# A hybrid of scan, attention and experts: the side products of the last attention loop are issued from two halves of one PSUM bank, in single bursts and at another pace

## The chip, the cores and the metric

The kernel runs on one core of a Trainium2 chip. The metric is the device time of one execution in microseconds (us). The engines are PE (TensorE: matrix products into PSUM), ACT (ScalarE), DVE (VectorE), POOL (GpSimd) and SP (SyncE, which issues most DMAs). PSUM has eight banks of 512 float32 columns in each of 128 partitions.

## The reference

Four images of 64 x 64 pixels and 128 channels pass through a state-space layer (three scans), then as 4096 tokens each through attention with a feed-forward part, then through experts that each pick tokens. What matters here comes after the scan:

```python
t = t + _L1_attn_ref(_ln_t(t), ...)        # (4, 4096, 128)
t = t + _L1_ffn_ref(_ln_t(t), ...)

# _L1_attn_ref: 16 heads of 8
scores = jnp.einsum('bhsd,bhtd->bhst', q, q) / np.sqrt(D)
attn = jax.nn.softmax(scores, axis=-1)
ctx = jnp.einsum('bhst,bhtd->bhsd', attn, q)
attn_out = ctx @ w_comb.T + b_comb
x1 = _ln(x + attn_out, g1, beta1)
zf = jnp.cos(x1[..., :8]) * jnp.cos(ry_theta)
h = jax.nn.relu(zf @ w1.T + b1)            # w1 (512, 8)
ffn_out = h @ w2.T + b2                    # w2 (128, 512)
return _ln(x1 + ffn_out, g2, beta2)

# _L1_ffn_ref: 64 experts, each picks K = 8 tokens of an image
logits = jnp.einsum('bsd,ed->bse', x, gate_w) + gate_b
probs = jax.nn.softmax(logits, axis=1)     # over the tokens
vals, idx = jax.lax.top_k(probs.transpose(0, 2, 1), K)
pooled = jnp.einsum('bked,bke->bed', gathered, topv)
# two layers per expert, weighted by topv, added to the picked tokens
```

## The kernel before

**Stages.** The scan of image 0 and the inputs of all images come first (the fill). Then attention runs image by image in four loops. Loops 0, 1 and 2 carry beside them the scan of the next image, its opening, and the closing (`after`) of the image before. The last loop has no scan left to carry. Behind it stand the closing of image 3's last block, the experts' choice for it, their answers and the scatter: the tail.

**A loop** has 1024 rounds: 32 turns (4 groups of heads by 8 blocks of 512 queries) of 32 rounds, one for each 128 keys. A round issues, in this order:
- `scores(i + 1)` (L1013): four float32r products on row tiles of 32 into two of the three two-bank tiles `s`, and two ACT exponentials of 128 x 1024 (L1018);
- `beside(i)`: side work;
- `values(i)` (L1027): four fp32 products on column tiles of 32 into the one bank `acc`.

Behind a turn's last round DVE copies `acc` to `av` (L1036), and three rounds later POOL issues the stores of the context and the sums. PSUM is full with that: six banks of scores, one `acc`, one `bank` for all side work.

**The order is written out by hand.** Each engine runs its own instructions in the order in which the program issues them, under `manual_schedule`. So a side product in PE's line whose input is late holds the values and scores behind it. Side work is a chain of generators. Each `yield PE` says that the next step is a product; `WAIT` says that a step can do nothing yet. `Pace.turn(share, free)` adds credit in each round and runs steps for it, at most one PE step a round, and none where `free` is false. The last loop's call is

```python
block.loop(nb - 1, lambda i: last.turn(1.5, i % 3 > 0 or i > 830), True)
```

`flow` keeps two pieces of work interleaved. A piece asks for PSUM with `Bank.take`, which yields `PE` once and then as long as the bank is taken; `leave` gives it back when the copy out has been issued. `pause` yields `PE` between two parts of a product, so that they stand in different rounds: a part is called a burst here, and one of two matmuls a double.

**Side work of the last loop**, in order: the closing of image 2, the choice of experts' tokens for images 0 and 1 and then 2, and the closing of image 3's first seven blocks as they become ready. A closing of a 512-token block has these products: `co` (combination of heads, L1130, 2 x 2 matmuls of 128 columns), `zt` (transpose of the cosines, L1153), `h` (first feed-forward product, L1171, 4 x 2 of 256 columns), `fo` (second, L1184, 4 x 4 of 128 columns, accumulating), `xT` (transpose, L1208) and `lg` (gate, L1222). In front of `co` stand the shares (`shares`: the sums of the exponentials are loaded, inverted, stored and loaded again) and behind `fo` two normalizations in a row (`norm`, L886 to L901). A `norm` is statistics on DVE, a power on POOL and four applications on DVE (L899); the second writes the tokens that `xT` transposes. DVE moves every product out of PSUM: h at L1174, fo at L1188. Between `co` and `zt` the cosines of all blocks of a group are formed: DVE folds the angles (`turned`), ACT takes the sine (L1241), for which it loads another function table and then the exponential's again. The choice (`choice`, L1315 to L1345) takes eight values of each row out of 4096, on DVE, in steps of some 4.4 us; the gathering (`pool`) then has for each block four `wt` matmuls (transposes weighted by the share, L1357) and four accumulating `pool` matmuls (L1368).

Of the kernel before, what the change touches and what calls it, by code (L numbers as in the profile page):

```python
# [11 lines left out]
F32 = mybir.dt.float32  # L12
# [114 lines left out]

class Bank:


# [14 lines left out]
    def leave(self):  # L145
        self.free += 1
# [582 lines left out]
class Attention:  # L729
# [3 lines left out]
    def __init__(self, tc, ctx, w, gate, cols, ident, bank, dram, t1, w_out, scans, sz, x):  # L733
# [16 lines left out]
        self.cos_ry = const.tile([D, 3], F32, name="cos_ry")  # L750
        nc.scalar.dma_start(out=self.cos_ry[:, 0:1], in_=w["ry_theta"].unsqueeze(1))
        cosine(nc, self.cos_ry[:, 2:3], self.cos_ry[:, 0:1], self.cos_ry[:, 1:2], self.half_pi)
        self.w_comb = const.tile([P, C], F32, name="w_comb")
        self.w1 = const.tile([D, FFN], F32, name="w1")
# [6 lines left out]
        with tc.tile_pool(name="a_load", bufs=1) as load, tc.tile_pool(  # L761
            name="a_load_ps", bufs=2, space=PSUM
        ) as load_ps:
            raw = load.tile([P, C], F32, name="raw_comb")
            nc.sync.dma_start(out=raw, in_=w["w_comb"])
            ps = load_ps.tile([P, 512], F32, tag="ps", name="ps_comb")
            nc.tensor.transpose(ps[:, :C], raw, ident)
            nc.vector.tensor_copy(self.w_comb, ps[:, :C])
            raw = load.tile([P, 4, D], F32, name="raw_w1")
            nc.sync.dma_start(out=raw, in_=w["w1"].rearrange("(f p) d -> p f d", p=P))  # L770
            ps = load_ps.tile([P, 512], F32, tag="ps", name="ps_w1")
            for f in range(4):
                nc.tensor.transpose(ps[:D, f * P : (f + 1) * P], raw[:, f, :], ident)
            nc.vector.tensor_copy(self.w1, ps[:D])
            raw = load.tile([P, FFN], F32, name="raw_w2")
            nc.sync.dma_start(out=raw, in_=w["w2"])
            ps = load_ps.tile([P, 512], F32, tag="ps", name="ps_w2")
            for f in range(4):
                nc.tensor.transpose(ps[:, f * P : (f + 1) * P], raw[:, f * P : (f + 1) * P], ident)
            nc.vector.tensor_copy(self.w2.rearrange("p f c -> p (f c)"), ps)  # L780
            raw = load.tile([E, C], F32, name="raw_gate")
            nc.scalar.dma_start(out=raw, in_=gate_w)
            ps = load_ps.tile([P, 512], F32, tag="ps", name="ps_gate")
            nc.tensor.transpose(ps[:, :E], raw, ident[:E, :E])
            nc.vector.tensor_copy(self.gate, ps[:, :E])
# [90 lines left out]
    def pause(self):  # L876

        if self.cut:
            yield PE

# [193 lines left out]
    def after(self, b, gs=range(L // QB), to=None):  # L1074
# [13 lines left out]
        z = self.small.tile([P, NT, D], F32, tag="z", bufs=1, name=f"z_{b}_{gs[0]}")  # L1088

# [20 lines left out]
        def first(g):  # L1110
# [15 lines left out]
            for half in range(2):  # L1126
                ps = yield from self.bank.take(f"co_{b}_{g}_{half}")
                for k in range(2):
                    at = slice((2 * half + k) * P, (2 * half + k + 1) * P)
                    nc.tensor.matmul(ps[:, k * C : (k + 1) * C], cT[:, at], self.w_comb, start=True, stop=True)  # L1130
                yield
                u_h = flat(u[:, 2 * half : 2 * half + 2, :])
                nc.vector.tensor_add(u_h, u_h, ps[:, : 2 * C])
                self.bank.leave()
# [8 lines left out]
        def second(g):  # L1143
# [5 lines left out]
            ps = yield from self.bank.take(f"zt_{b}_{g}")  # L1149
            for k in range(4):  # L1150
                if k == 2:
                    yield from self.pause()
                nc.tensor.transpose(ps[:D, k * P : (k + 1) * P], z[:, g * 4 + k, :], self.ident)  # L1153
            yield
            zT = self.piece([D, 512], "p0", name=f"zT_{b}_{g}")
            nc.vector.tensor_scalar_mul(zT, ps[:D], self.cos_ry[:, 2:3])
            self.bank.leave()
# [7 lines left out]
            for f in range(4):  # L1165
                ps = yield from self.bank.take(f"h_{b}_{g}_{f}")
                for part in range(2):
                    cols = slice(part * QB // 2, (part + 1) * QB // 2)
                    if part:
                        yield from self.pause()  # L1170
                    nc.tensor.matmul(ps[:, cols], self.w1[:, f * P : (f + 1) * P], zT[:, cols], start=True, stop=True)  # L1171
                yield
                if self.n == 2:
                    nc.vector.tensor_scalar(h[:, f, :], ps, self.b1[:, f : f + 1], 0.0, ALU.add, ALU.max)  # L1174
                else:
                    nc.scalar.activation(h[:, f, :], ps, AF.Relu, bias=self.b1[:, f : f + 1])
                self.bank.leave()
            yield from self.settle()
            for k in range(4):
                ps = yield from self.bank.take(f"fo_{b}_{g}_{k}")  # L1180
                for f in range(4):
                    if f == 2:
                        yield from self.pause()
                    nc.tensor.matmul(  # L1184
                        ps[:, :C], h[:, f, k * P : (k + 1) * P], self.w2[:, f, :], start=(f == 0), stop=(f == 3)
                    )
                yield
                nc.vector.tensor_add(u[:, k, :], u[:, k, :], ps[:, :C])  # L1188
                self.bank.leave()
# [14 lines left out]
            ps = yield from self.bank.take(f"xT_{b}_{g}")  # L1204
            for k in range(4):
                if k == 2:
                    yield from self.pause()
                nc.tensor.transpose(ps[:, k * P : (k + 1) * P], u[:, k, :], self.ident)  # L1208
            yield
            xT = self.piece([P, 512], "p0", name=f"xT_{b}_{g}")  # L1210
            nc.vector.tensor_copy(xT, ps)  # L1211
            self.bank.leave()
# [3 lines left out]
            ps = yield from self.bank.take(f"lg_{b}_{g}")  # L1216
            rows = slice(E, 2 * E) if to else slice(0, E)
            for part in range(2):
                cols = slice(part * QB // 2, (part + 1) * QB // 2)
                if part:  # L1220
                    yield from self.pause()
                nc.tensor.matmul(ps[rows, cols], self.gate, xT[:, cols], start=True, stop=True)  # L1222
            yield
            if to:
                for t in to:
                    nc.vector.tensor_scalar_add(t, ps[rows], self.gate_b[rows])
            else:
                lg = self.piece([E, 512], "p1", name=f"lgs_{b}_{g}")
                nc.vector.tensor_scalar_add(lg, ps[rows], self.gate_b[rows])
                nc.gpsimd.dma_start(out=self.logits[b][:, g * 512 : (g + 1) * 512], in_=lg)  # L1230
            self.bank.leave()
# [3 lines left out]
        def cosines():  # L1235
            turns = self.small.tile([P, NT, D], F32, tag="zturns", bufs=1, name=f"zturn_{b}_{gs[0]}")
            zs, turns = (t[:, 4 * gs[0] : 4 * blocks.stop, :] for t in (z, turns))
# [4 lines left out]
            yield  # L1242
            yield
# [10 lines left out]
class Experts:  # L1254
# [4 lines left out]
    def __init__(self, tc, ctx, ident, weight1, weight2, block, nb):  # L1259
# [14 lines left out]
        self.diagonal = const.tile([P, nb // 2, E], F32, name="diagonal")  # L1274
        self.found, self.ahead, self.rooms = {}, [], 0

    def biases(self):
# [13 lines left out]
        bank.leave()  # L1291
# [23 lines left out]
    def choice(self, images, blocks):  # L1315
# [24 lines left out]
        for b in images:  # L1340
            own = slice(b % 2 * E, b % 2 * E + E)
            nc.vector.tensor_scalar_mul(
                self.diagonal[own, b // 2, :], self.ident[own, own], self.share[own, b // 2 : b // 2 + 1]
# [4 lines left out]
    def pool(self, b, g):  # L1348

        nc, bank, rows = self.nc, self.block.bank, slice(b % 2 * E, b % 2 * E + E)  # L1350
        x = self.some.tile([P, 4, C], F32, tag="x", bufs=4, name=f"x_{b}_{g}")
        nc.sync.dma_start(out=x, in_=self.block.xn[b][:, g * 4 : g * 4 + 4, :])
        yield
        ps = yield from bank.take(f"wt_{b}_{g}")
        for i in range(4):
            at = (g * 4 + i) * P
            nc.tensor.matmul(  # L1357
                ps[:, i * E : (i + 1) * E], self.chosen[b // 2][rows, at : at + P], self.diagonal[rows, b // 2, :],
                start=True, stop=True,
            )  # L1360
        yield
        wT = self.some.tile([P, 4, E], F32, tag="wT", name=f"wT_{b}_{g}")
        nc.vector.tensor_copy(wT.rearrange("p i e -> p (i e)"), ps[:, : 4 * E])
        bank.leave()
        yield
        ps = yield from bank.take(f"pool_{b}_{g}")
        for i in range(4):
            nc.tensor.matmul(ps[:, :E], x[:, i, :], wT[:, i, :], start=(i == 0), stop=(i == 3))  # L1368
        yield
        into = self.pooled[:, :, b]  # L1370
        if g == 0:
            nc.vector.tensor_copy(into, ps[:, :E])
        else:
            nc.vector.tensor_add(into, into, ps[:, :E])
        bank.leave()
        yield

    def gather(self, images):
        yield from flow((self.pool(b, g) for b in images for g in range(NT // 4)), 2, 3)
# [157 lines left out]
def tile_kernel(tc, ctx, x, in_proj_w, dirs, out_proj_w, attn, gate, weight1, weight2, out):  # L1537
# [86 lines left out]
    with tc.manual_schedule():  # L1624
# [9 lines left out]
        block.loop(nb - 1, lambda i: last.turn(1.5, i % 3 > 0 or i > 830), True)  # L1634
# [52 lines left out]
```

## Time and profile before

| | us |
|---|---|
| median of three runs | 11369.05 |
| lowest, highest | 11349.99, 11371.47 |
| the profiled execution: time | 11359.39 |
| its span (first to last instruction) | 11357.7 |
| loop 0, from its first exponential to its last | 1997 to 4375 |
| loop 1 | 4379 to 6740 |
| loop 2 | 6747 to 9070 |
| last loop | 9073 to 11108 |
| tail | 11108 to 11358 |

The mean granted clock of PE is 0.943 of full speed. A row of the profile's groups reads: line of the kernel, engine, operation, result and operands, their shapes, count, then busy time in all, mean nanoseconds of one, and the idle time of the engine ahead of it with what ended most of it. A row of the timeline reads: start and length in us, engine, line, operation, and in brackets how long the engine had been idle and what released it. The ends of matmuls are modelled, so neighbouring rows on PE overlap a little. An fp32 matmul is recorded twice, because it is done in two passes; a float32r matmul or a transpose is recorded once.

### The profile page before, as it was taken

The page shows a single profiled execution, that of the slowest core. Times are in us where ns is not written, and L with a number is a line of the kernel's source. Part 1 is how long each engine was busy: PE and PEld are TensorE (multiplying, and loading weights), DVE is VectorE, ACT ScalarE, POOL GpSimd, SP SyncE. Part 2 cuts the span into 40 slices and gives each one's busy share as a digit, 9 for nine tenths or more (in the row PEclk, how much of TensorE's full clock was granted, in tenths as well). Part 3 has the DMA queues.
Part 4 walks back from the last instruction along what each step waited for, and adds up shares of the span by engine and source line. Part 5 has one row for each costly group of instructions (what it writes and reads, how often), then busy time and mean ns, then how long its engine had stood idle before and what let it go on. Part 6 is the DMA issues. An engine that isn't in the chain of part 4 may idle for free.

```text
span 11357.7 us, 182956 instructions
## 1 busy us (share of the span) xinstructions
PE 9864.2 (87%) x68358; PEld 3270.5 (29%) x68358; DVE 8267.2 (73%) x8405; ACT 9991.9 (88%) x10828; POOL 3757.7 (33%) x3891
## 2 busy tenths in 40 slices
PE   6697782888999889999998898999998999999995
PEld 2233331222222222222222222222222223333323
DVE  7999987888888987999998979988999221111212
ACT  4576672999999999999999999999999999989992
POOL 5887773323323223334233124243331110000000
PEclk8898895999999999999999999999999999999997
DMA  7888887556566665665656655656555332222225
GB/s 200 235 253 228 231 239 206 147 144 156 140 155 164 178 171 140 158 164 136 156 140 172 185 158 153 156 140 153 148 146 156 119 99 71 76 71 83 76 64 187
DMA packets 900978, 1747.50 MB, mean 154 GB/s; under 512 B 203150, under 2 KB 443846, under 8 KB 899830
## 3 DMA queue, kind: packets, MB, share of 16 engines
q1 hardware_dynamic: 764414, 1468.11, 48.4%
q0 software_dynamic: 93856, 156.41, 4.8%
q10 hardware_dynamic: 41816, 111.28, 3.4%
q8 instruction: 537, 8.80, 0.3%
q14 instruction: 355, 2.91, 0.1%
HBM read 1379.76 MB, written 355.47 MB: 153 GB/s over the span
## 4 chain that ended last, share of the span: by engine, by line
PE 37%; ACT 25%; issue 14%; DVE 12%; DMA 10%; POOL 1%; SPq 1%; ACTq 0%; DVEq 0%; POOLq 0%
PE acc L1027 21%; ACT e L1018 20%; PE s L1013 10%; DVE h L576 5%; DMA delta<-d_delta 4%; DMA du<-d_du 2%; PE cv L415 2%; DVE dB L566 1%; ACT dA L557 1%; ACT delta L557 1%; PE y L614 1%; PE fo L1184 1%; PE h L1171 1%; PE xd L431 1%; DMA B<-d_bc 0%
## 5 line engine op out<-in xcount | busy, mean ns | idle before, releaser
L1018 ACT ACTIVATE e<-s 128x1024 f32<-128x1024 f32 x8192 | 7777.9, 1105 | 233.1 <-PE s L1013 221.3
L1027 PE MATMUL acc<-e,val 128*32 128x512 f32 x32768 | 5255.2, 616 | 106.7 <-ACT av L1036 94.0
L1013 PE MATMUL s<-qm,key 32*128 32x512 f32 x16384 | 2648.4, 500 | 588.5 <-ACT e L1018 558.4
L1013 PEld LDWEIGHTS s<-qm,key 32*128 32x128 f32 x16384 | 1013.8, 184 | 4448.8 <-issue 2490.0
L578 POOL COPY ends<-h 128x1 f32<-128x1 f32 x1152 | 1292.6, 1123 | 2332.1 <-DVE h L576 2318.1
L566 DVE TENSOR_TENSOR dB<-du,B 128x1024 f32<-128x1024 f32 x960 | 1216.0, 1267 | 450.8 <-PE y L614 224.7
L1027 PEld LDWEIGHTS acc<-e,val 128*32 128x32 f32 x32768 | 972.6, 109 | 1608.4 <-issue 787.9
L576 DVE TENSOR_TENSOR_SCAN h<-dA,ends,dB 128x1024 f32<-128x1024 f32 x576 | 1350.4, 2344 | 110.9 <-ACT dA L557 70.7
L557 ACT ACTIVATE dA<-delta,A 128x1024 f32<-128x1024 f32 x768 | 935.6, 1218 | 421.4 <-DMA delta<-d_delta 373.7
L576 DVE TENSOR_TENSOR_SCAN h<-delta,ends,du 128x1024 f32<-128x1024 f32 x432 | 1012.3, 2343 | 127.4 <-ACT delta L557 64.8
L583 POOL TENSOR_TENSOR hC<-h,C 128x1024 f32<-128x1024 f32 x384 | 1001.1, 2608 | 160.2 <-PE y L614 85.1
L557 ACT ACTIVATE delta<-delta,A 128x1024 f32<-128x1024 f32 x768 | 937.4, 1221 | 21.6 <-DMA d_du<-u 7.1
L587 DVE TENSOR_TENSOR du<-h,C 128x1024 f32<-128x1024 f32 x576 | 701.1, 1217 | 0.1
L587 DVE TENSOR_TENSOR dB<-h,C 128x1024 f32<-128x1024 f32 x576 | 701.0, 1217 | 0.0
L566 DVE TENSOR_TENSOR du<-du,B 128x1024 f32<-128x1024 f32 x576 | 690.6, 1199 | 6.0 <-DMA B<-d_bc 5.9
L1042 POOL DMA_DIRECT2D d_ctx<-av x512 | 260.2, 518 | 1020.8 <-DVE av L1036 647.0
L415 PE MATMUL cv<-xn,conv 128*128 128x512 f32 x1024 | 472.6, 615 | 41.8 <-DVE xn L346 31.7
L608 POOL DMA_DIRECT2D d_du<-x_delta x272 | 157.2, 578 | 1012.9 <-DVE x_delta L607 951.8
L576 DVE TENSOR_TENSOR_SCAN h<-dA,dB 128x1024 f32<-128x1024 f32 x192 | 438.7, 2285 | 40.7 <-ACT dA L557 30.4
L614 PE MATMUL y<-dB,sel 128*32 128x256 f32 x4608 | 378.5, 401 | 9.5 <-DVE xT L1211 5.1
L576 DVE TENSOR_TENSOR_SCAN h<-delta,du 128x1024 f32<-128x1024 f32 x144 | 328.8, 2283 | 67.4 <-issue 34.5
L614 PE MATMUL y<-hC,sel 128*32 128x256 f32 x3072 | 239.8, 443 | 147.9 <-DVE o L630 144.6
(246 smaller groups left out, 7198.1 us busy)
## 6 DMA issues: line engine op xcount, KB each, us to landing
delta<-d_delta SPq DMA_DIRECT2D x768, 512.0 KB
du<-d_du SPq DMA_DIRECT2D x632, 512.0 KB
key<-d_q SPq DMA_DIRECT2D x352, 256.0 KB
du<-d_du ACTq DMA_DIRECT2D x136, 512.0 KB
B<-d_bc SPq DMA_DIRECT2D x96, 512.0 KB
C<-d_bc SPq DMA_DIRECT2D x96, 512.0 KB
us<-d_u SPq DMA_DIRECT2D x384, 128.0 KB
y<-d_y SPq DMA_DIRECT2D x192, 256.0 KB
```

Source lines behind the costliest of these rows:

```text
L415: nc.tensor.matmul(banks[2 * m + g], w["conv"][:, k, m * P : (m + 1) * P], reads(k, g), start=(k == 0), stop=(k == 3))
L557: nc.scalar.activation(tiles["delta", s], t, AF.Exp, scale=A)
L566: nc.vector.tensor_mul(tiles["du", s], du, spread[order, c, "B", j % 2])
L576: nc.vector.tensor_tensor_scan(h, dA, dB, first, ALU.mult, ALU.add)
L578: nc.gpsimd.tensor_copy(ends[order, c][:, at : at + 1], h[:, T - 1 :])
L583: nc.gpsimd.tensor_mul(tiles["du", s], h, spread[order, c, "C", j % 2])
L587: nc.vector.tensor_mul(dB, h, spread[order, c, "C", j % 2])
L614: nc.tensor.matmul(y[32 * g : 32 * g + 32, : T // 4], self.sel[:, j // 2, :], hC[:, 256 * g : 256 * g + 256], start=(j == 0), stop=(j == 3),)
L1013: nc.tensor.matmul(s_ps[:, k, :], keys[f"{i // 4}"][rows, cut].bitcast(F32R), queries[j, qb][rows, :].bitcast(F32R), start=True, stop=True,)
L1018: nc.scalar.activation(e, s_ps, AF.Exp, scale=1.0 / math.sqrt(D))
L1027: nc.tensor.matmul(accs[j, qb][32 * k : 32 * k + 32, :], v[:, k * VW : k * VW + 32], es[i][k // 2][:, k % 2, :], start=(kc == 0), stop=(kc ...
L1042: nc.gpsimd.dma_start(out=self.context[b][h * D : h * D + D, cut], in_=av[32 * k : 32 * k + D, :])
```

## The change

- In the last loop the side work gets `Halves` for its bank: one PSUM tile of 512 columns, handed out as two halves of 256. `take` yields `WAIT` (no longer `PE`) while no half is free, and while an accumulation is open (`summing`). `WAIT` doesn't use the PE step of a round.
- Bursts are single matmuls: `fo` pauses after each of its four matmuls, `co` and `wt` too. `pool` pauses once, after two.
- `h` becomes a float32r product with 32 rows: both factors are split into a high and a low part by a mask on the bits, and the four products of the parts are summed by one matmul of 32 rows. The weights are split at the start. The cosines are split behind ACT's sine in `cosines`, with cos(ry_theta) multiplied in there rather than at the copy of `zt`: four more DVE operations and one more `yield`. `zt` transposes 32 columns for each token tile. With a bank of 512 columns (loops 1 and 2, and the tail) one such matmul makes all of a 512-token block's `h` for 128 rows; with halves, two of 256.
- The two images of a pair are gathered together: `wt` is one matmul of 128 rows and 128 columns against a block-diagonal matrix (for a single image 64 by 64), and `pool` follows for each image.
- The pace of the last loop is 2.0 credits a round, with a PE step allowed in three rounds of four (all after 830).

The diff, cut:

```diff
 class Bank:
+    width, summing = 512, False
...
-    def leave(self):
+    def leave(self, ps=None):
+        self.free += 1
+
+class Halves(Bank):
+    width = 256
+
+    def __init__(self, whole):
+        self.parts, self.free = [whole[:, :256], whole[:, 256:]], 2
+
+    def take(self, name):
+        while True:
+            while not self.free or self.summing:
+                yield WAIT
+            yield PE
+            if self.free and not self.summing:
+                return self.grab(name)
+
+    def grab(self, name):
+        self.free -= 1
+        return self.parts.pop(0)
+
+    def leave(self, ps=None):
+        self.parts.append(ps)
         self.free += 1
...
-    def pause(self):
+    def pause(self, fresh=False):
         if self.cut:
             yield PE
+            while fresh and self.bank.summing:
+                yield WAIT
+                yield PE
...
                 for k in range(2):
+                    if k:
+                        yield from self.pause(True)
                     at = slice((2 * half + k) * P, (2 * half + k + 1) * P)
                     nc.tensor.matmul(ps[:, k * C : (k + 1) * C], cT[:, at], self.w_comb, start=True, stop=True)
...
             for f in range(4):
-                ps = yield from self.bank.take(f"h_{b}_{g}_{f}")
-                for part in range(2):
-                    cols = slice(part * QB // 2, (part + 1) * QB // 2)
-                    if part:
-                        yield from self.pause()
-                    nc.tensor.matmul(ps[:, cols], self.w1[:, f * P : (f + 1) * P], zT[:, cols], start=True, stop=True)
-                yield
-                if self.n == 2:
-                    nc.vector.tensor_scalar(h[:, f, :], ps, self.b1[:, f : f + 1], 0.0, ALU.add, ALU.max)
...
+                for col in parts_of:
+                    ps = yield from self.bank.take(f"h_{b}_{g}_{f}_{col.start}")
+                    nc.tensor.matmul(
+                        ps[:, :width], self.w1[:, f * P : (f + 1) * P].bitcast(F32R), zT[:, col].bitcast(F32R),
+                        start=True, stop=True,
+                    )
+                    yield
+                    if self.n == 2:
+                        nc.vector.tensor_scalar(h[:, f, col], ps[:, :width], self.b1[:, f : f + 1], 0.0, ALU.add, ALU.max)
...
                 for f in range(4):
-                    if f == 2:
+                    if f:
                         yield from self.pause()
+                    self.bank.summing = f < 3
...
         def cosines():
...
             nc.scalar.activation(zs, zs, AF.Sin, bias=self.half_pi, scale=-1.0)
             yield
+            yield
+            n = zs.shape[1]
+            four = parts[:, 4 * gs[0] : 4 * blocks.stop, :, :]
+            nc.vector.tensor_mul(zs, zs, self.cos_ry[:, 2, :].unsqueeze(1).to_broadcast([P, n, D]))
+            split(nc, (four[:, :, 0, :], four[:, :, 1, :]), zs)
+            nc.vector.tensor_copy(four[:, :, 2:, :], four[:, :, :2, :])
             yield
...
-    def pool(self, b, g):
+    def pool(self, images, g):
...
+        own = min(4, bank.width // n)
+        for first in range(0, 4, own):
+            ps = yield from bank.take(f"wt_{images[0]}_{g}_{first}")
+            for i in range(own):
+                at = (g * 4 + first + i) * P
+                if i:
+                    yield from pause(True)
+                nc.tensor.matmul(
+                    ps[:, i * n : (i + 1) * n], self.chosen[j][rows, at : at + P], self.diagonal[rows, j, rows],
+                    start=True, stop=True,
+                )
...
+            for i in range(4):
+                if i == 2:
+                    yield from pause()
+                bank.summing = i < 3
+                nc.tensor.matmul(ps[:, :E], x[:, i, :], wT[:, i, k * E : (k + 1) * E], start=(i == 0), stop=(i == 3))
...
-        block.loop(nb - 1, lambda i: last.turn(1.5, i % 3 > 0 or i > 830), True)
+        block.bank = Halves(bank.pool.tile([P, 512], F32, tag="bank", name="halves"))
+        block.loop(nb - 1, lambda i: last.turn(2.0, i % 4 > 0 or i > 830), True)
```

`zt`, `xT` and `lg` are cut the same way: by halves of 256 columns, each with its own `take`, copy and `leave`.

## The prediction

> **What bounds the kernel now.** First the page, for what bounds the loops:
>
> ```profile
> PE 9864.2 (87%) x68358; PEld 3270.5 (29%) x68358; DVE 8267.2 (73%) x8405; ACT 9991.9 (88%) x10828; POOL 3757.7 (33%) x3891
> ...
> L1018 ACT ACTIVATE e<-s 128x1024 f32<-128x1024 f32 x8192 | 7777.9, 1105 | 233.1 <-PE s L1013 221.3
> ```
>
> PE and ACT are level over the span, so it is the stage that tells. The table of windows over the last loop (PE, PEld, DVE, ACT, POOL busy, then clock, DMA share, GB/s):
>
> ```profile
> 9073.00:11108.00 2035.00, 1963.13 (x13692) 631.74 (x13688) 393.44 (x995) 1925.52 (x2079) 177.08 (x314) 0.98 0.26 76
> ```
>
> PE's busy here contains pipelined ends, so it is not the bound by itself. ACT's exponentials are: from the start of one round's pair to the next, the median of rounds without side work is 1.825 us. PE needs less, as its timeline shows (start, length):
>
> ```profile
> 9331.04 0.59 PE L1171 MATMUL h<-zT,w 8*128 8x256 f32 x2
> 9331.56 1.07 PE L1027 MATMUL acc<-e,val 128*32 128x512 f32 x8
> 9332.56 0.51 PE L1013 MATMUL s<-qm,key 32*128 32x512 f32 x4
> 9332.99 0.71 PE L1184 MATMUL fo<-w,h 128*128 128x128 f32 x4
> 9333.64 1.06 PE L1027 MATMUL acc<-e,val 128*32 128x512 f32 x8
> 9334.63 0.50 PE L1013 MATMUL s<-qm,key 32*128 32x512 f32 x4
> 9335.06 1.21 PE L1027 MATMUL acc<-e,val 128*32 128x512 f32 x8
> ```
>
> Scores to values is 0.43 us without a burst, 1.08 with an fo double; values to the next scores 1.00. So a round needs 1.43 us of PE, its slack against 1.825 is about 0.4, and a burst costs only what exceeds that. The loop's 1023 rounds take 2034.7 us: 166 us over 1023 x 1.825. Medians of the rounds by what they carry: h single 1.847, fo double 2.065 (mean 2.025), co double 2.04, lg single 1.97, four wt 2.40, four pool 2.41, zt and xT doubles 1.83. With their counts (120 h, 120 fo, 30 co, 30 lg, 24 wt, 24 pool) that is 2.6 + 25 + 6.6 + 4.4 + 13.8 + 13.9, about 66 us. The other 100 us are ACT's side work (choice, sines, table loads: the same after) and rounds in which PE waits for a side product's input. The groups of this loop (busy, mean ns, idle before):
>
> ```profile
> L1184 PE MATMUL fo<-w,h 128*128 128x128 f32 x480 | 85.4, 300 | 0.0
> L1171 PE MATMUL h<-zT,w 8*128 8x256 f32 x240 | 72.2, 379 | 4.8 <-DVE h L1174 4.6
> L1357 PE MATMUL wt<-diagonal,chosen 64*128 64x64 f32 x192 | 28.2, 290 | 9.5 <-DVE chosen L1345 8.9 <-DVE pooled L1372 0.6
> ...
> L1208 PE MATMUL xT<-ident,x1r 128*128 128x128 f32 x60 | 14.4, 323 | 15.1 <-DVE x1r L899 15.1
> ```
>
> The price of such a wait is in the timeline (idle before, releaser in brackets):
>
> ```profile
> 9771.07 0.69 PE L1171 MATMUL h<-zT,w 8*128 8x256 f32 x2 [3.19 <-DVE h L1174]
> ...
> 9773.14 1.05 PE L1171 MATMUL h<-zT,w 8*128 8x256 f32 x2
> 9774.12 1.93 PE L1027 MATMUL acc<-e,val 128*32 128x512 f32 x8
> ```
>
> The h product stands in PE's line ahead of values and scores, so everything waits; and after 3.19 us of idleness values that take 1.06 above take 1.93. The three rounds here are 3.6, 1.6 and 0.8 us too long: 6.0 us for 3.19.
>
> **The change part by part.**
>
> *Single bursts.* 120 fo doubles become 240 singles, 30 co doubles 60. A single is two passes of 128 columns; the nearest row is an xT double, two transposes of 128 columns in 0.44 us, whose rounds are at +0.00. I take 0.02 (lower 0, upper 0.09, under half of the double's mean excess of 0.20): 25 + 6.6 becomes about 6, **-26** (-5 to -32). *wt and pool.* 24 bursts of four wt become 64 singles, no larger than fo's: 13.8 to about 1, -13. 24 of four pool become 48 of two, half of 1.10 us in PE's line; between 0 and the fo double's 0.24, I take 0.15: 13.9 to 7, -7. *h and lg.* h becomes one float32r pass of 256 columns where fp32 took two: -2.6. lg stays. Sum **-48**.
>
> Here a rule of the Trainium skill speaks against the change: "TensorEngine Tiling (Array Packing)", Key Properties, says that changing the tiling mode drains TensorE, and rounds with a burst rise from 409 to 623. In the trace h, which shares the scores' 32-row tile, starts 0.34 us after the scores and fo 0.43, so a switch is about 0.1 us; on 214 more rounds that would be +21 if paid in full. The xT doubles switch twice and cost nothing measurable, so I keep +0, because the slack hides it; a round with another delay would pay.
>
> *Two halves of one bank.* In the changed order every product into either half still waits for the latest DVE copy out of the other, and copies wait for later products. So the halves give turns, not overlap of PE and DVE. What they and pace 2.0 (for 1.5 per round, three rounds of four for two of three) change is distance: a pair of feed-forward blocks takes 44 rounds for 51, and PE comes to products sooner after what DVE must finish first. DVE's chain behind a block's last fo:
>
> ```profile
> 9373.32 0.29 DVE L1188 TENSOR_TENSOR x1r<-x1r,fo 128x128 f32<-128x128 f32 x1 [5.51 <-PE fo L1184]
> ...
> 9382.33 0.18 DVE L894 BATCH_NORM_AGGREGATE mv_x<-st_x 128x2 f32<-128x6 f32 x1
> 9383.94 0.35 DVE L899 TENSOR_SCALAR x1r<-t,mv_x,rs_x 128x128 f32<-128x128 f32 x1 [1.43 <-POOL rs_x L51]
> ```
>
> The second normalization's statistics end 9.2 us after the fo copy starts; an h copy queued there ends at 9.6, the applications at 11.8. Stalls after, from the rounds between producer and product in the built order:
> - *h*: in nine blocks the second h stands 4 rounds after the last fo (139 to 143, for one), with its predecessor's copy behind the chain. It has 4 x 1.83 less 0.7 = 6.6 us, and 9.6 are needed: 3.0 idle. Price from both sides: 2.7 (idle less slack) and 6.0 (the stall shown). I take 4.5, since 3.0 is nearest to 3.19 but some will miss the slow clock. Nine are 40; one at a turn's end behind the copy of acc adds 5.5, another 0.9. Before, such rounds cost about 13: **+34** (+18 to +47).
> - *xT* after the chain with one flow: 3 rounds for 4, four times; one round less is at most +1.8 each, taken 1.6 on the 5.3 of before: **+6**.
> - *co* behind the sum of shares (load, 3.35 us reciprocal, store, load, about 10.5 us): 4 rounds for 6 and 5, twice: **+4.5**; its own chain of waits **+2**.
> - *wt* behind the choice, 3 rounds for 4, and acc's copy behind the choice's 4.4 us steps at two turns' ends: **+5**.
> - *Sines* come 3 rounds after the last co, for 4 or 5, so ACT waits 1 to 2 us for DVE's folding, four times: **+6**; the four extra DVE operations (cosine of ry, split) run after ACT's part and precede only zt: 0 to +4, taken 0.
>
> Sum of stalls **+57**. They are priced by what the trace shows of the clock; this row bears on it:
>
> ```profile
> 9943.20:9945.80 2.60, 2.60 (x16) 0.50 (x15) 0.04 (x1) 0.00 (x0) 0.60 (x1) 0.50 0.46 179
> ```
>
> After a 4.24 us wait of xT the granted clock is 0.50. The skill's "TensorE: Matmul & The Clock Gate", Part 1, has the clock halve after at least one idle window of about 3.4 us, windows running free. By it nine idles of 3.0 us stay warm, 24 us, and the whole sum is 16 lower; by the row, where 3.19 us was enough, it is up to 54. I stay between, nearer to the row.
>
> *Queues.* SP issues the loads of x for pool two at a time, ahead of wt as before; POOL's stores of context, mid and xn keep their places behind DVE's results. No row of this loop has PE waiting for a load of x, so they are at 0; cover is the several rounds between load and product.
>
> *Other stages.* In loops 1 and 2, rounds with an h burst have a median of 2.86 against 2.85 without: ACT's scan exponentials hide a shorter h, and the order of waits stays; 0 (-4 to +4). In the tail 16 h products take 7.19 us, ahead of ACT's four relus; as four single passes the relus bound it: **-3**. Splitting w1 at the start adds four DVE operations of at most 32 elements; an aggregate of 128x2 takes 0.18, so below 1, taken 0.
>
> **Sum**: -48 + 57 - 3 = +6 on the profiled run's 11359.4 (span 11357.7), 11366. That run is 9.7 below the median 11369; on the median it is 11375.
>
> **The rivals.** 0.2%, some 23 us, is what a measurement of this kernel can tell from no change.
> 1. *Bursts become free and waits don't grow.* For: singles fit the 0.4 us; idles of 3.0 just miss the clock's fall. Against: the built order puts h 4 rounds behind the chain. The nine stalls at 2 us or less and half of the smaller ones: h at 18 + 6 - 13 = +11, the rest +12, so -48 + 23 - 3 = -28, and -51 with no new wait: 11318 to 11346, typically **11341**.
> 2. *Slower: the h product behind the normalization.* Place: the second h after each block's last fo. Price: 6.0 us as at 9771 for nine, +54 for 40; and if a single fo costs 0.09, 240 of them give back 17. +6 + 14 + 17 = +37: **11406**. It decides, at 23 us over no change, once a stall costs over 5.3 us with singles at 0.06, or 6.4 with singles at 0.02.
> 3. *The halves don't do what they say*: one bank, one wait at a time. The order shows this already; it is within the likeliest case, which has no overlap in it. If the copy of a half also delayed each next single, rival 2 results.
>
> **How the numbers follow.** Likeliest: gain and new waits cancel, 0.43, 11346 to 11392, at 11375. Faster, rival 1: 0.22. Slower, rival 2: 0.35. The range leaves out a tenth on each side: 11328 to 11415.
>
> **What would show it.** Right: fo and co singles with means near 300 ns and zero excess, rounds with fo under 1.86; idle before h grown from 4.6 to some 25 to 35 us, released by DVE's h copy; xT's idle near 20; last loop 2030 to 2055 us; mean clock in it a little below 0.98; tail 3 us shorter. Wrong: h's idle under 12 (rival 1), or fo's rounds above 1.9 (rival 2); loops 1 and 2 moved by over 8 us would mean that their order, taken as neutral, isn't.

## Result and the profile after

The changed kernel takes 11403.7 us (median of seven, 11397.5 to 11412.9) for 11363.9 of the kernel before (seven, 11350.0 to 11371.5): a ratio of 1.0037, 95% interval 1.0025 to 1.0049, so 40 us slower by the medians and 42 by the ratio. It lies in the forecast range; the likeliest case (no change, 11375) is not what came. The profiled execution has a span of 11411.2 us.

The table of windows over the last loop and the tail (PE, PEld, DVE, ACT, POOL busy, clock, DMA share, GB/s), of the changed kernel:

```profile
9078.90:11167.20 2088.30, 1938.34 (x13494) 601.68 (x13494) 411.96 (x1116) 1912.54 (x2078) 177.32 (x314) 0.95 0.25 75
11167.20:11411.00 243.80, 122.03 (x1158) 87.66 (x1154) 74.85 (x158) 32.28 (x52) 25.74 (x47) 0.66 0.61 212
```

The last loop, counted here to the start of its last round, grew by 55.6 us (2032.7 before) and the tail shrank by 7.6. Loops 0, 1 and 2 moved by some 2 us or less each, the fill by 5, which is within what the fill varies among the kernels below. PE's busy time fell by 22 us and its granted clock from 0.98 to 0.95: PE does less, stands still more, and comes back slower. The groups of the last loop show both (busy, mean ns, idle before and releaser):

```profile
L1235 PE MATMUL halves<-w,h 128*128 128x128 f32 x480 | 117.2, 326 | 0.0
L1176 PE MATMUL halves<-w_comb,cT 128*128 128x128 f32 x120 | 34.9, 379 | 49.9 <-DVE x L1179 33.5 <-DVE cT L1166 16.4
L1218 PE MATMUL halves<-zT,w 32*128 32x256 f32 x120 | 34.7, 289 | 22.9 <-DVE h L1224 22.9
L1433 PE MATMUL halves<-wT,x 128*128 128x64 f32 x192 | 31.6, 287 | 0.0
...
L1261 PE MATMUL halves<-ident,x1r 128*128 128x128 f32 x60 | 15.3, 343 | 24.1 <-DVE x1r L942 24.1
```

Here L1176 is co, L1218 h, L1235 fo, L1433 pool, L1261 xT. The row of co in the kernel before is

```profile
L1130 PE MATMUL co<-w_comb,cT 128*128 128x128 f32 x120 | 22.6, 313 | 13.6 <-DVE x L1133 7.4 <-DVE cT L1122 6.1
```

Idle before co rose from 13.6 to 49.9 us, before h from 4.6 to 22.9, before xT from 15.1 to 24.1. The bursts themselves became nearly free, as the timeline of two rounds with an fo single shows; scores follow scores after 1.85 us:

```profile
9311.49 0.51 PE L1056 MATMUL s<-qm,key 32*128 32x512 f32 x4
9311.92 0.49 PE L1235 MATMUL halves<-w,h 128*128 128x128 f32 x2
9312.34 1.06 PE L1070 MATMUL acc<-e,val 128*32 128x512 f32 x8
9313.34 0.51 PE L1056 MATMUL s<-qm,key 32*128 32x512 f32 x4
9313.78 0.49 PE L1235 MATMUL halves<-w,h 128*128 128x128 f32 x2
```

Counted by rounds, against the quiet 1.825 us: rounds that are at most 1 us too long add up to 33.0 us, for 67.9 before (-35). Rounds over that add up to 188.4, for 97.9 (+90.5), by kind: co +47; behind the copy of acc +12; h +19; xT +12; wt -1; ACT's sines and choices +1.5.

Much of co's part falls at the loop's start. The last co of image 2 stands in round 54 in both kernels. At the start of that round the changed one is 40.8 us behind (154.0 for 113.1 us from the loop's start), but the kernel before has its last wait of co, 4.24 us, still to come in this round. At the start of the next round it is 34.9 behind, at round 80, behind the sines of image 2, 35.4 (207.5 for 172.1), and at the end 55.6. Round 80 is the place to compare the kernels below, because their co phases end in rounds 42 to 72. One of those waits, PE's timeline and then that of SP and DVE:

```profile
9132.17 0.50 PE L1056 MATMUL s<-qm,key 32*128 32x512 f32 x4
9138.46 0.80 PE L1176 MATMUL halves<-w_comb,cT 128*128 128x128 f32 x2 [5.79 <-DVE x L1179]
```

```profile
9129.45 0.18 DVE L1185 COPY z<-x 128x32 f32<-128x32 f32 x1
...
9133.02 0.55 SPq L1161 DMA_DIRECT2D part<-d_share  x1
...
9137.38 0.69 DVE L1166 TENSOR_TENSOR cT<-cT,part 128x512 f32<-128x512 f32 x1 [7.74 <-DMA part<-d_share]
9137.99 0.41 DVE L1179 TENSOR_TENSOR x<-x,halves 128x256 f32<-128x256 f32 x1
```

A co product needs the bank, the bank needs the copy out of the other half (0.41 us), and that copy stands in DVE's line behind the next block's multiplication by its shares, which waits 7.74 us for a load (SP issues it at 9133.02). PE and DVE stand still over this, and ACT too once it has used up its scores, at 9134.8.

### The profile page after: what moved, and what is told of

Same layout as the page of the kernel before. It is cut to its first block, busy times and chain, and to the rows that moved or that the text cites. A ratio compares the mean times of both kernels' runs of the same rounds, so it can differ in the third digit from the quotient of the medians.

```text
span 11411.2 us, 182234 instructions
## 1 busy us (share of the span) xinstructions
PE 9820.9 (86%) x67936; PEld 3208.2 (28%) x67936; DVE 8288.5 (73%) x8542; ACT 9981.1 (87%) x10828; POOL 3766.0 (33%) x3891
## 4 chain that ended last, share of the span: by engine, by line
PE 36%; ACT 23%; issue 14%; DVE 13%; DMA 11%; POOL 1%; SPq 1%; ACTq 0%; DVEq 0%; POOLq 0%
PE acc L1070 20%; ACT e L1061 19%; PE s L1056 10%; DVE h L610 5%; DMA delta<-d_delta 3%; DMA du<-d_du 2%; PE cv L449 2%; DVE dB L600 2%; ACT dA L591 1%; ACT delta L591 1%; PE halves L1235 1%; PE y L648 1%; DMA d_y<-o 1%; PE xd L465 1%; DVE du L621 1%
## 5 line engine op out<-in xcount | busy, mean ns | idle before, releaser
L648 PE MATMUL y<-du,sel 128*32 128x256 f32 x4608 | 362.4, 387 | 0.0
```

The source lines that it names most:

```text
L648: nc.tensor.matmul(y[32 * g : 32 * g + 32, : T // 4], self.sel[:, j // 2, :], hC[:, 256 * g : 256 * g + 256], start=(j == 0), stop=(j == 3),)
```

## The experiments

Four tell pace from parts, four follow from them. The kernel before was timed again beside them and took 11355.1 us with the first four and 11362.4 with the last four; the ratios go by these times, so they compare better than the times do. What is said by rounds and waits is read from one trace of each kernel.

**The pace alone undone.**

```diff
-        block.loop(nb - 1, lambda i: last.turn(2.0, i % 4 > 0 or i > 830), True)
+        block.loop(nb - 1, lambda i: last.turn(1.5, i % 3 > 0 or i > 830), True)
```

> The changed kernel with one line undone: the pace of the last loop is again 1.5 credits a round with a PE step in two rounds of three. Halves, single bursts, the float32r product and the gathering by pairs stay. Theory P (pace): the last loop grew by 55.6 us because 2.0 credits bring PE to products whose DVE and DMA chain is not done; with the old pace PE's waits for side products (now 107 us by the profile's list of co, xT, h and wt) fall to 50 or less and the last loop ends near 1975 to 2000 us for 2088. Part of the side work then runs on behind the loop, 20 to 40 us, so the total is about 11310 to 11350. Theory H (halves): the waits come from the two halves being one bank, where each product waits for the copy out of the other half, and from co in four turns for two; then the waits stay above 90 us at any pace, the co phase of image 2 is still some 40 us longer than before, and the total is 11390 or more.

Measured: 11380.1 us, ratio to before 1.0025 (1.0015 to 1.0035). The windows of loop and tail:

```profile
9062.20:11040.90 1978.70, 1905.88 (x13387) 587.65 (x13387) 370.55 (x999) 1905.16 (x2075) 166.35 (x295) 0.98 0.24 76
11040.90:11379.00 338.10, 156.54 (x1265) 110.34 (x1261) 116.57 (x275) 32.59 (x53) 37.14 (x66) 0.62 0.49 169
```

The loop is 1978.7, as theory P said: 54 us below before. PE's waits for side products are 37 us; at round 80 the kernel is 1.6 us behind the one before, for 35.4. But the total is above the band of theory P, because the cost of the work left over was taken too low: the tail is 338 us for 252, where 20 to 40 more were expected. Single bursts need more rounds, and at the old pace they do not fit into the loop. In the tail, DVE, PE and ACT pass this work on to each other with nothing beside it. So the pace makes the stalls, and it is also what the parts needed in order to end in time.

**The pace alone done**, on the kernel before (the same two values in its call).

> The kernel before with the new pace alone: 2.0 credits a round, a PE step in three rounds of four. One bank of 512 columns, doubles, fp32 h. Theory P: the stalls appear without any halves: the last loop grows from 2033 by 60 to 100 us, total 11425 to 11465, with PE waiting for co's cT and x, h and xT. Theory H: the pace by itself only moves work forward; the last loop stays within 15 us of 2033.

Measured: 11422.6 us, 2 us under the band, ratio 1.0061 (1.0046 to 1.0076); the last loop is 2099.4 us (+66.7), the tail unchanged. At round 80 it is 18.4 us behind. PE's list of waits in that loop (sum, times, longest), of this kernel:

```profile
PE co L1130 <- DVE cT L1122: 24.7, 8, 9.6
PE xT L1208 <- DVE x1r L899: 24.2, 4, 6.1
PE co L1130 <- DVE x L1133: 21.4, 10, 4.8
...
PE acc L1027 <- DVE av L1036: 12.3, 27, 2.6
PE wt L1357 <- DVE chosen L1345: 11.7, 2, 6.5
PE h L1171 <- DVE h L1174: 8.0, 8, 3.8
```

The same waits come without halves and without singles: theory P holds, and theory H, by which the pace alone would change next to nothing, falls. Waits of h are fewer here (8.0 for 22.9): that part needs something of the changed parts as well (not fo's singles: with fo in doubles, below, h waits 22.5).

**co in doubles again**, at 2.0.

```diff
-                    if k:
-                        yield from self.pause(True)
```

> The changed kernel with co in doubles again: the pause between the two matmuls of a half is left out, all else as changed. By the trace the co phase of image 2 (to round 54) is 40.8 us longer than before. If the four turns of co for a block cause it, the phase shrinks by 30 us or more and the total falls to about 11370. If the cause is the pace (theory P), the two phases differ by little: the 16 doubles cost 0.2 us each more, a few waits fall away, and the total is 11390 to 11405.

Measured: 11382.4 us, ratio 1.0025 (1.0016 to 1.0035); last loop 2069.9, tail 241.1. At round 80 it is 19.2 us behind the kernel before, for 35.4, and PE's waits of co are 36.6 us for 49.9. So at this pace the four turns of co account for 16 us of the phase, neither for 30 nor for next to nothing; the other 19 are about what the pace alone did to the kernel before (18.4). At the old pace the same four turns cost next to nothing (1.6): it is the two together.

**fo in doubles again**, at 2.0 (`if f == 2` for `if f` ahead of the pause).

> The changed kernel with fo in two doubles a sum for four singles, all else as changed. What the singles bring by themselves: 120 doubles at +0.20 us against 240 singles measured at +0.02, so by the sum of bursts this is 20 us slower. The rounds freed (two fewer for each sum) also bring later products nearer to their producers, so with theory P the stalls grow and it is 25 to 40 us slower, about 11430 to 11445. If a single's switch of tile mode were what costs (a drain in 120 more rounds), this would be faster, near 11380.

Measured: 11443.9 us, ratio 1.0084 (1.0067 to 1.0101); last loop 2139.0 (+50.7 on the changed kernel). Rounds up to 1 us too long rise from 33.0 to 55.4: the singles are worth 22 us, as the sum of bursts had it. The other 28 us are stalls: PE's waits for the copy of acc rise from 27.0 to 42.2 us, those of co from 49.9 to 59.7. That fewer PE steps put products nearer to their inputs is the likely reason; no run shows it apart. The total is in the band, and a gain from fewer mode switches did not show.

**No load of shares in the co phase**, at 2.0.

```diff
-            part = self.piece([P, 512], "p1", name=f"part_{b}_{g}")
-            nc.sync.dma_start(
-                out=part, in_=share[g - gs[0]].unsqueeze(1).to_broadcast([H, D, 512])
-            )
...
-            nc.vector.tensor_mul(cT, cT, part)
```

> The changed kernel at its pace of 2.0 without the multiplication of the context by the shares and without the load of the shares for it (the output lacks the division by the sum of exponentials). DVE then has no operation in the co phase that waits for a DMA, and co reads the loaded context. If co's new waits are DVE standing at that load with the copies of the other piece behind it, the co phase of image 2 shrinks from 154.0 us by 25 to 35, PE's waits of co from 50 to 25 us or less, and the total falls to 11365 to 11385. If they are the copies of the two halves waiting for each other and the normalization chain, the phase stays within 10 us and the total above 11390. h's and xT's waits (23 and 24 us) stay in both.

Measured: 11362.8 us, ratio to before 1.0001 (0.9992 to 1.0010), that is 41 us below the changed kernel and just below the band expected. At round 80 it is 5.0 us behind, for 35.4. The list of waits in its last loop:

```profile
PE halves L1256 <- DVE x1r L942: 24.1, 4, 6.1
PE halves L1213 <- DVE h L1219: 23.9, 10, 2.8
PE halves L1171 <- DVE x L1174: 22.7, 7, 4.3
PE acc L1070 <- DVE av L1079: 21.1, 26, 4.9
...
PE halves L1171 <- DMA cT<-d_ctx: 3.4, 1, 3.4
```

co's waits fall from 49.9 to 26.1 (22.7 and 3.4), those of xT (first line) and h (second) stay. So 30 of the 35.4 us go with that load, at which DVE stands. They overlap with the 16 us of co's four turns, so the two can't be added. The multiplication's own 0.69 us per block is gone too, 5.5 us over the eight blocks of image 2; this run does not separate that from the wait.

**1.65 and 1.75 credits**, a PE step in three rounds of four as in the change.

> The changed kernel at 1.65 credits a round, with the PE step in three rounds of four kept. At 1.5 (and two of three) the last loop took 1978.7 us but 86 us of side work ran on in the tail; at 2.0 it took 2088.3 with nothing left over. If the stalls come from pace and not from the parts, there is a point between: co's and h's waits stay near those at 1.5 (27 and 8 us), the last loop is 1970 to 2000 us, hardly anything is left for the tail (250 to 270 us for 244), and the total is 11300 to 11340, below both kernels. If stalls rise evenly with the pace, the last loop is near 2010 and the total near 11350.

> The changed kernel at 1.75 credits a round, PE step in three rounds of four. A second point on the same line. If the stalls set in by a step, when the rounds between a product and its input fall below the chain of DVE (h four rounds after the last fo), h's waits are here already as at 2.0 (some 23 us) while co's are not (20 for 50), and the last loop is 2020 to 2050, the total 11340 to 11370. If they rise evenly, the last loop is near 2035 with h and co both at half.

Measured: at 1.65, 11328.0 us, ratio 0.9968 (0.9956 to 0.9980); at 1.75, 11364.9, ratio 1.0002 (0.9993 to 1.0011). The windows of the last loop at 1.65 and its tail, and then the first of PE's waits at 1.75:

```profile
9075.90:11060.90 1985.00, 1906.96 (x13481) 596.23 (x13480) 397.88 (x1082) 1907.45 (x2077) 172.71 (x307) 0.98 0.25 77
11060.90:11326.00 265.10, 124.90 (x1170) 89.39 (x1170) 89.00 (x192) 32.15 (x52) 30.05 (x54) 0.66 0.59 206
```

```profile
PE halves L1218 <- DVE h L1224: 28.8, 12, 2.7
PE acc L1070 <- DVE av L1079: 20.7, 26, 7.3
PE halves L1261 <- DVE x1r L942: 18.2, 3, 6.1
```

At 1.65 loop, tail and total are all in the bands of the first expectation, a point between the two paces below both kernels. (In the last loop alone, co's and h's waits at the old pace are 19 and 5 us; the 27 and 8 named there take in part of the tail.) h's waits go from 0.9 us (one, at 1.65) to 28.8 (twelve, of up to 2.74 each), more than at 2.0, while co's stay at 25 and 21. A wait of 0.92 grown by one round of 1.83 is 2.74: a product comes a whole round nearer to its input or not at all, so these waits set in by a step. The loop at 1.75, 2032, fits both expectations and does not tell them apart.

**1.65 and co in doubles.**

> The changed kernel at 1.65 credits a round, and co in doubles again. With 30 steps of PE less, no side product should be left for the tail, which then takes about 241 us as with co doubles at 2.0. The doubles cost 30 x 0.2 = 6 us of bursts. If co's singles bring nothing beyond that, the last loop is as at 1.65 plus 5 to 10, and the total is within 10 us of it, 11300 to 11340; if the singles' waits for the other half matter even at this pace, it is 10 to 20 us faster.

Measured: 11311.4 us, ratio 0.9953 (0.9940 to 0.9965), the fastest here, 0.5% below before.

```profile
9079.30:11067.30 1988.00, 1908.76 (x13494) 600.59 (x13494) 411.80 (x1116) 1910.12 (x2077) 176.40 (x314) 0.98 0.26 78
11067.30:11312.00 244.70, 121.87 (x1158) 87.90 (x1155) 75.11 (x158) 32.32 (x52) 25.76 (x47) 0.67 0.61 212
```

It is 17 us better than 1.65 alone, but not for the reason that the second expectation named: the loop is 3 us longer, and 20 us come from the tail, where nothing is left over.

All of them side by side; "waits" is PE's idle time in the last loop for anything but the exponentials, the sum of its list:

| kernel | credits | last loop | tail | waits | clock | ratio |
|---|---|---|---|---|---|---|
| before | 1.5 | 2032.7 | 252 | 53.6 | 0.98 | 1 |
| before, pace | 2.0 | 2099.4 | 253 | 102.3 | 0.97 | 1.0061 |
| changed | 2.0 | 2088.3 | 244 | 133.0 | 0.95 | 1.0037 |
| fo doubles | 2.0 | 2139.0 | 244 | 152.4 | 0.95 | 1.0084 |
| co doubles | 2.0 | 2069.9 | 241 | 116.3 | 0.96 | 1.0025 |
| no shares | 2.0 | 2046.7 | 241 | 102.9 | 0.96 | 1.0001 |
| 1.75 | 1.75 | 2032.3 | 249 | 96.2 | 0.97 | 1.0002 |
| 1.65 | 1.65 | 1985.0 | 265 | 63.0 | 0.98 | 0.9968 |
| 1.65, co doubles | 1.65 | 1988.0 | 245 | 63.4 | 0.98 | 0.9953 |
| old pace | 1.5 | 1978.7 | 338 | 60.6 | 0.98 | 1.0025 |

Between the old pace and the changed kernel the loop gains 109.6 us for 72.4 us of waits: 1.5 us for each. Part of that is work which the old pace leaves to the tail. On the kernels with the changed parts it holds to within 8 us: from 1978.7 with that slope, 1.75 would be 2032 (measured 2032.3), no shares 2042 (2046.7), co doubles 2062 (2069.9), and fo doubles 2116, or 2138 with their 22 us of bursts (2139.0). Taken from the changed kernel, whose loop holds about the same work as these, it is 1.1 us for each in co doubles (18.4 for 16.7), 1.4 in no shares and 1.5 at 1.75.

## Why the prediction was right or wrong

The range held, and the direction that the sum leaned to (+6 us) is the one measured; the size did not. The last loop, 2088 us, is outside the 2030 to 2055 that were to show the prediction right. That the total still lies in the range is in part luck: the term of co was 40 us too small, while those of h, wt, the sines and the tail were together some 25 too large. The difference of spans is +53.5: last loop +55.6, tail -7.6, fill and the loops before it +5.5.

- *What bounds, and the slack of 0.4 us a round*: right. (The 2034.7 us given for 1023 rounds contain the last round's exponentials; the 166 us of excess belong to 2032.7.) Rounds with fo singles have a mean of 1.842 us (+0.017; 0.02 was taken), h singles a median of 1.829, pairs of pool 1.961 (+0.136; 0.15). The sum of bursts was put at -48; in the rounds up to 1 us too long it shows as -35. Part of what the 24 bursts of four wt cost stood in rounds that also stalled, and can't be told apart there.
- *Mode switches*: +0 was right. 623 rounds with a burst in place of 409, and no such cost in fo's singles.
- *Halves give no overlap*: confirmed by the waits of co for the copy out of the other half. The wait stands in the program itself: a product into one half carries a semaphore of the copy out of the other. Whether the chip would need it, no run shows.
- *h behind the normalization*: the mechanism is right almost to the digit, the price too high. The chain at round 143 and PE's line there:

```profile
9402.17 0.29 DVE L1239 TENSOR_TENSOR x1r<-x1r,halves 128x128 f32<-128x128 f32 x1 [8.89 <-PE halves L1235]
...
9411.27 0.45 DVE L1224 TENSOR_SCALAR h<-halves,b 128x256 f32<-128x256 f32 x1
```

```profile
9411.78 0.58 PE L1218 MATMUL halves<-zT,w 32*128 32x256 f32 x1 [2.74 <-DVE h L1224]
9412.29 1.94 PE L1070 MATMUL acc<-e,val 128*32 128x512 f32 x8
```

  The h copy ends 9.55 us after the fo copy starts (9.6 predicted) and PE idles 2.74 (3.0). These rounds came out 2.7 to 4.1 too long, where 4.5 was taken for each. With the copy of acc behind the chain (5.5 at round 97, as predicted) the term is some +24 for +34. Rival 2 gave the right total (11406) in the wrong place: its 6.0 us at each h is not there.
- *xT*: one round less gave idles of 6.0 us for 4.24, and rounds 7.5 too long for the 6.9 predicted: +12 for +6.
- *co*: the step that failed. "*co* behind the sum of shares [...] **+4.5**; its own chain of waits **+2**" is +6.5; measured +47, and more where the copy of acc waits in the same phase. Some +12 of it are behind the shares and some +36 are co's own chain, products that wait for the copy out of the other half. For the +2 the prediction gives no working. The co phase of image 2 ends in the same round in both kernels, but the order within had changed, and the runs show what that costs: with the same parts at the old pace the kernel is only 1.6 us behind at round 80, at 2.0 without the load of shares 5.0, with co in doubles 19.2, as built 35.4. The prediction followed the built order for h block by block; for co it did so behind the sum of shares alone, and not where a DMA's landing stands in DVE's line ahead of a copy that PE needs.
- *wt and the sines*: +11 predicted, about 0 measured.
- *Tail*: -7.6 for -3. The four h products now take 2.07 us for 7.19 and ACT makes its four relus in one run. PE's line before and after, and ACT's after:

```profile
11147.37 7.19 PE L1171 MATMUL h<-zT,w 8*128 8x256 f32 x16 [0.83 <-DVE zT L1156]
...
11205.81 2.07 PE L1218 MATMUL h<-zT,w 32*128 32x512 f32 x4 [0.77 <-DVE zT L1206]
```

```profile
11206.69 2.42 ACT L1226 ACTIVATE h<-h,b 128x512 f32<-128x512 f32 x4 [3.63 <-PE h L1218]
```

  From the start of zt to the last relu's end it is 5.1 us (11204.0 to 11209.1), 4.7 less than before. Where the other 3 us come from stays open.

Some versions were not run and stay open: 1.5 credits with the PE step in three rounds of four (below 1.65 the two values of the pace changed together), a slower pace for the first 70 rounds alone, and empty steps ahead of xT, whose waits (16.8 us at 1.65 with co doubles) are the largest left.

## What to carry to other kernels

When side work is issued by hand into the gaps of a bound loop, making its pieces cheaper and issuing them sooner are two changes: the first was worth 35 us here; the second lengthened the loop by 67 us on the kernel before, and by 110 on the changed one, whose tail gave 94 back. Count for each product the rounds since its last input was issued, against the time of the chain between, and do so first where a DMA stands in that chain; the step at which waits set in is sharp (h: one wait of 0.9 us at 1.65 credits, twelve of 28.8 in all at 1.75). The slowest pace that still ends inside the loop is the one to seek: from 1.65 to the old pace the loop won 6 us more, and the tail, with nothing beside it, lost 73.

## What was not expected of the hardware

A wait of PE costs more than its length: 1.1 to 1.5 us of loop for each us waited, by the pairs above. One reason is the clock that PE is granted behind it. In the last loops of the ten traces any two changes of this clock are a whole number of windows of 3.413 us apart, to a few ns. Two pauses of equal length, 2.74 us up to 9411.78 (round 143) and 2.75 us up to 9835.93 (round 363), lie differently in these windows (a row gives the stretch, its length and PE's busy time first, and the clock third from the end):

```profile
9407.48:9410.90 3.42, 1.56 (x12) 0.33 (x8) 3.20 (x10) 3.42 (x5) 0.61 (x1) 1.00 0.00 0
9410.90:9417.72 6.82, 5.94 (x29) 1.47 (x33) 2.30 (x9) 2.28 (x4) 1.81 (x3) 0.50 0.20 79
```

```profile
9830.75:9834.16 3.41, 2.44 (x19) 0.77 (x17) 3.24 (x9) 3.41 (x4) 0.07 (x1) 1.00 0.02 5
9834.16:9837.57 3.41, 1.64 (x13) 0.53 (x13) 2.25 (x11) 1.15 (x2) 1.76 (x3) 1.00 0.34 112
9837.57:9840.98 3.41, 3.41 (x20) 0.69 (x20) 0.88 (x3) 2.45 (x3) 0.60 (x1) 0.50 0.34 129
```

Of the first pause 1.86 us fall into one window, and from its end the clock is 0.50 for two windows: the values behind the pause take 1.94 us. The second is split, 0.98 and 1.77 us. The first window changes nothing, the second halves the clock from 9837.57 for one window; so the first values still take 1.07 us and only the next 1.94, and this round was 2.8 us too long for 4.1. The same count over the ten loops, by the profile's busy time, whose ends are modelled: all 196 windows at full clock in which PE idled for 1.8 us or more were followed by half the clock, 28 of the 100 with 1.2 to 1.8 us, and none with less. So what counts here is the idle time inside one window, about half of it, and not the length of a pause. The Trainium skill's "TensorE: Matmul & The Clock Gate", Part 1, has free-running windows of about 3.4 us, with which these traces agree, and a fall of the clock after at least one idle window, where in these traces about half of one was enough. The 3.19 us that the prediction went by put 1.6 us into the window that halved the clock.
